# Splitting the first tap additions of a dynamic filter between GpSimd and VectorE

## The chip, the cores and the metric

The kernel runs on one core of a Trainium2 chip. Its metric is the device time of one execution in microseconds (us). The core's engines work beside each other, each through its own list of instructions in order: TensorE (PE; its weight loads stand apart as PEld), VectorE (DVE), ScalarE (ACT), GpSimd (POOL) and the queue SP, which here only issues DMAs. They wait for one another by semaphores. SBUF is the working memory; PSUM is the memory that TensorE writes[...].

## The reference: two layers on four images

The input is four images of 256 channels and 48 x 48 pixels in fp32. Layer 0 adds to each image the result of a 3x3 convolution, batch norm, ReLU and an attention over all 2304 pixels with eight heads. Layer 1 is what the change touches:

```python
def _dyn_branch(x, w, d):
    xp = jnp.pad(x, ((0, 0), (0, 0), (d, d), (d, d)))
    out = jnp.zeros_like(x)
    k = 0
    for dy in (-d, 0, d):
        for dx in (-d, 0, d):
            patch = xp[:, :, d + dy:d + dy + H, d + dx:d + dx + W]
            out = out + patch * w[:, k:k + 1]
            k += 1
    return out
guidance = _conv(x, W_cat, pad=1)
outs = [x]
for i, d in enumerate((1, 6, 12, 24, 36)):
    w = jax.nn.softmax(guidance[:, 9 * i:9 * (i + 1)], axis=1)
    outs.append(_dyn_branch(x, w, d))
y = _conv(jnp.concatenate(outs, axis=1), W_scale, pad=0)
```

So every pixel has 45 weights of its own: nine taps for each of five dilations. A tap is the image, shifted, times a weights map that is the same for all channels. The taps of a dilation are added, and a 1x1 convolution mixes the image and the five sums. A batch norm over all images follows.

## The kernel before

A tile has 128 partitions. The 256 channels are two halves of 128, which lie behind each other in a tile: a chunk of 8 image rows, 384 pixels, is 2 x 384 = 768 numbers in each partition. An image has six chunks.

The program runs image by image. The attention of an image (L951 to L1030) is followed by a stage in which `dynamic_filters` computes layer 1 of that image, while the convolution and the projections of the *next* image (L739 to L921) are mixed in between, where TensorE would else wait. There are four such stages; the last has no next image, and there the flag `alone` is set.

In a stage, each tap of a chunk goes through three engines:

- The weights map of the tap is spread over all 128 partitions into a PSUM bank, `wb`. TensorE does it with a matmul (L1384), or ScalarE copies a map that a DMA has spread (L1381). There are three such banks, five in the last stage.
- VectorE multiplies the bank with the shifted image, both halves at once. The first tap of a dilation, `at == 0`, is written straight into the sum, `cat` (L1407). Every other tap goes into one of five product buffers, `prod` (L1417), which exist so that VectorE can run ahead of GpSimd. The bank is then free.
- GpSimd adds the product to `cat`, both halves at once (L1434). The product buffer is then free.

When the last tap of a dilation has been added, TensorE mixes `cat` into the output `py` (L1280). Taps at the image's edge are smaller: with dilation 6, a tap that is shifted sideways has 42 of 48 columns, 2 x 8 x 42 = 672 numbers.

In the last stage, a product may also skip GpSimd: TensorE then mixes the product itself (`single`).

The order of all instructions is set while the program is being built. A small model, `clock`, keeps a planned time for each engine; every instruction adds its planned cost. `slot` says when a buffer comes free by that model. From these times the planner decides whether TensorE or ScalarE spreads a map, when a queued mixing matmul is due, how much of the next image's convolution goes in between (`fill`), and in the last stage which products are `single`. The planned cost of a GpSimd add is `added`. On the chip, the engines then keep that order, whatever the true times are.

Of the kernel before, what the change touches and what calls it, by code (L numbers as in the profile page):

```python
# [8 lines left out]
F32 = mybir.dt.float32  # L9
F32R = mybir.dt.float32r  # L10
AF = mybir.ActivationFunctionType
ALU = mybir.AluOpType
# [3 lines left out]
B, C, HH, WW = 4, 256, 48, 48  # L16
N = HH * WW
P = 128
NH = C // P
# [4 lines left out]
CH = R * WW  # L24
# [12 lines left out]
CATS = 4  # L37
PRODS = 5
SLACK = 3000.0
BEHIND = 0.0  # L40


# [5 lines left out]
def conv_preact_kernel(  # L48
# [12 lines left out]
    nc = tc.nc  # L61
# [73 lines left out]
    def window(gn, h, r0, dy, dx):  # L135

        return gn[:, h, 1 + r0 + dy : 1 + r0 + dy + R, 1 + dx : 1 + dx + WW]
# [393 lines left out]
    with tc.tile_pool(name="w", bufs=1) as wpool, tc.tile_pool(  # L531
        name="act", bufs=1
# [122 lines left out]
        clock = Clock()  # L655
        free = {}

        def slot(tag, bufs):

            ends = free.setdefault(tag, [])  # L660
            return ends[-bufs] if len(ends) >= bufs else 0.0
# [438 lines left out]
        def dynamic_filters(b, ao, chunk, norm, other, pools):  # L1100


            ps_w, ps_y, ps_m, work1 = pools
# [3 lines left out]
            def misc(name):  # L1107
                return ps_m.tile([P, 512], F32, tag="misc", name=name)
# [134 lines left out]
            def fill(until):  # L1243

                while clock.t["PE"] < until:
# [5 lines left out]
                    if queue and when(queue[0]) <= clock.t["PE"]:  # L1251
                        queue.pop(0)[-1]()
                        continue
                    if spent[0] > spread[0] + SLACK:
                        return
# [86 lines left out]
            for c in range(NCK):  # L1342
                if alone and c == 1:
                    back()
                if c in plan:
                    for _ in ahead:
                        pass
                    if alone and c == 2:
                        flag_of(misc("pf")[:1, : B * NH])
                    ahead = weights(plan[c])  # L1350
                    pace = [0.0, 0, 0.0]

                    due = plan[c][0] - c
                while c not in ready:
                    next(ahead)
                for o in range(NH):
                    queue.append(
                        (0.0, "", mix(c, 0, o, lambda i, c=c: window(gn, i, c * R, 0, 0)))
                    )
                w = ready[c]  # L1360
                taps = [
                    (n, at, t) for n in range(len(DILATIONS)) for at, t in enumerate(taps_of(c, n))
                ]
                for j, (n, at, (k, oy, ox, y0, y1, x0, x1)) in enumerate(taps):
                    if at == 0:
                        mixed("cat", NH * (CATS - 1))
                        cat = work1.tile(
                            [P, NH, CH], F32, tag="cat", name=f"cat_{b}_{c}_{n}", bufs=CATS
                        )
                    catv = cat.rearrange("p h (r w) -> p h r w", w=WW)  # L1370
                    nr, ncol = y1 - y0, x1 - x0
                    l0, l1 = y0 - c * R, y1 - c * R
                    fill(slot("wb", 5 if alone else 3))
                    pw = ps_w.tile([P, 512], F32, tag="w", name=f"wb_{b}_{c}_{k}")
                    spot = slot("wb", 5 if alone else 3)
                    if (c, k) in number:
                        fetch(number[c, k] + WBS)
                        of, there = landed[c, k]
                        late = max(clock.t["ACT"], spot + 150, there + 150) + 300
                    if (c, k) in number and late <= max(clock.t["DVE"], clock.t["PE"], spot + 150):  # L1380
                        nc.scalar.copy(pw[:, : nr * WW], of[:, : nr * WW])  # L1381
                        given = clock("ACT", nr * WW + 100, slot("wb", 5 if alone else 3), there)
                    else:
                        nc.tensor.matmul(  # L1384
                            pw[:, : nr * WW],
                            pick[:, k : k + 1].to_broadcast([P, P]),
                            w[:, l0 * WW : l1 * WW],
                            start=True,
                            stop=True,
                        )  # L1390
                        given = clock("PE", 0.45 * nr * WW + 20, slot("wb", 5 if alone else 3))
                    wb = (
                        pw[:, : nr * WW]
                        .rearrange("p (r w) -> p r w", w=WW)[:, :, x0:x1]
                        .unsqueeze(1)
                        .to_broadcast([P, NH, nr, ncol])
                    )
                    src = gn[:, :, 1 + y0 + oy : 1 + y1 + oy, 1 + x0 + ox : 1 + x1 + ox]
                    ns = NH * nr * ncol
                    ns, added = 1.05 * ns + 150, 2.1 * ns + (190 if ncol == WW else 80)  # L1400

                    single = (
                        alone and at > 0
                        and clock.t["POOL"] + added > clock.t["PE"] + len(queue) * NH * MM + BEHIND
                    )
                    if at == 0:
                        nc.vector.tensor_tensor(catv, wb, src, ALU.mult)  # L1407
                        end = summed = clock("DVE", ns, given)
                    else:
                        if single:  # L1410
                            mixed("single", 2 * NH)
                        tag, bufs = ("single", 3) if single else ("prod", PRODS)
                        prod = work1.tile(
                            [P, NH, CH], F32, tag=tag, name=f"prod_{b}_{c}_{k}", bufs=bufs
                        )
                        pv = prod[:, :, : nr * ncol].rearrange("p h (r w) -> p h r w", w=ncol)
                        nc.vector.tensor_tensor(pv, wb, src, ALU.mult)  # L1417
                        end = clock(
                            "DVE", ns, given, 0.0 if single else slot("prod", PRODS)
                        )  # L1420
                    free["wb"].append(end)
                    if single:
                        for o in range(NH):
                            queue.append((
                                end + 150, "single",
                                mix(
                                    c, n + 1, o,
                                    lambda i, t=prod, m=nr * ncol: t[:, i, :m],
                                    at=(l0, l1, x0, x1),
                                ),  # L1430
                            ))
                    elif at:
                        dst = catv[:, :, l0:l1, x0:x1]
                        nc.gpsimd.tensor_tensor(dst, dst, pv, ALU.add)  # L1434
                        summed = clock("POOL", added, end)
                        free["prod"].append(summed)
                    spread[0] += spread[1] * NH * nr * ncol
                    pace[0] += STEPS * 1.15 * NH * nr * ncol * NCK / due / TAP_ELEMENTS
                    if j + 1 == len(taps) or taps[j + 1][0] != n:
                        for o in range(NH):  # L1440
                            queue.append((
                                summed + 150, "cat",
                                mix(
                                    c, n + 1, o, lambda i, cat=cat: cat[:, i, :],
                                    n == len(DILATIONS) - 1,
                                ),
                            ))
# [96 lines left out]
        for b in range(B + 1):  # L1544

            with tc.tile_pool(name=f"work1_{b}", bufs=2) as work1, tc.tile_pool(
                name=f"ps_c_{b}", bufs=2, space=PSUM
            ) as ps_c, tc.tile_pool(
                name=f"ps_w_{b}", bufs=5 if b == B else 3, space=PSUM
            ) as ps_w, tc.tile_pool(  # L1550
                name=f"ps_y_{b}", bufs=1, space=PSUM
# [71 lines left out]
                else:  # L1623
                    if b == B:
# [24 lines left out]
                        def back():  # L1649

                            for bb, ty, tx in ((0, y_0, x1_0), (1, y_1, x1_1), (2, None, x1_2)):
                                if ty is not None:
                                    nc.sync.dma_start(out=ty, in_=y_d[bb])
                                nc.sync.dma_start(out=tx, in_=x1_d[bb])
                            for c, t in enumerate(y_2):
                                nc.sync.dma_start(out=t, in_=chunk_of(y_d, 2, c))
# [42 lines left out]
            with tc.tile_pool(name=f"work0_{b}", bufs=2) as work0, tc.tile_pool(  # L1699
                name=f"ps_s_{b}", bufs=3, space=PSUM  # L1700
# [3 lines left out]
                    lambda c, ao, pp, b=b, n=norm1: project(b, c, ao, pp, n), scratch,  # L1704
# [76 lines left out]
```

## Time and profile before

Three runs took 2962.0, 2967.0 and 2967.2 us. The profiled execution's span is 2967.9 us, at a mean granted TensorE clock of 0.979.

| what | instructions | busy, us | mean, ns |
|---|---|---|---|
| whole span: PE | 16967 | 2791.2 | |
| whole span: DVE | 2412 | 2390.4 | |
| whole span: ACT | 2103 | 1674.9 | |
| whole span: POOL | 1022 | 1253.5 | |
| L1434, adds on POOL | 740 | 996.5 | 1357 |
| L1417, products on DVE | 768 | 553.1 | 746 |
| L1407, first taps on DVE | 120 | 113.8 | 948 |
| L1384, maps spread by PE | 629 | 293.0 | 501 |
| L1381, maps spread by ACT | 259 | 121.2 | 468 |
| L1280, mixing of `cat` on PE | 960 | 349.6 | 496 |

The table gives busy time. A busy engine is not yet the one that sets the pace, and a share of the whole span is a mean over stages of different kinds: the four layer 1 stages lie at 559 to 854, 1277 to 1571, 1990 to 2281 and 2692 to 2930 us, some 38% of the span, and between them lie the attentions. So the questions are asked of one such stage: which engine is busy in it nearly without a gap, and who waits for whom. Matmuls are pipelined and their ends in the record are modelled, so for PE the distance from start to start says more than the busy time. The mean of a line mixes shapes of different sizes; a cost is read from the rows that keep shapes apart.

### The profile page before, as it was taken

To read this page: it belongs to the slowest core of one execution; us is meant where nothing else is said; L and a number is where in the kernel's file an instruction comes from. 1 tells how busy PE (TensorE), PEld (TensorE's weight loads), DVE (VectorE), ACT (ScalarE), POOL (GpSimd) and SP (SyncE) were. 2 spreads that over 40 slices of the span, in tenths; PEclk is the share of its full clock that TensorE was granted. 3 is DMA by queue.
4 is the path that set the end of the run, shared out by engine and by line. 5 is a ranking of instruction groups with operands and counts; after the bars stand their busy time and mean duration, and the time that the engine had idled before them with its cause. 6 is when DMAs were issued, how large, how long until landed. Compare 5 with 4: busy or idle time off the path is not lost. (4 is left out here: it accounts for less than half of the span.)

```text
span 2967.9 us, 43643 instructions
## 1 busy us (share of the span) xinstructions
PE 2791.2 (94%) x16967; PEld 1248.9 (42%) x16967; DVE 2390.4 (81%) x2412; ACT 1674.9 (56%) x2103; POOL 1253.5 (42%) x1022
## 2 busy tenths in 40 slices
PE   7999999999989999999899999999998999998994
PEld 5622224556542222455562222355555222244552
DVE  6388999779758899877976899977885999986776
ACT  3489888322348988711236988852133888871124
POOL 1010000898840010299791000069986100006994
PEclk9999999999999999999999999999999999999997
DMA  4422333222252333322225333223213333335225
GB/s 177 99 66 65 66 75 70 66 72 85 68 121 65 63 77 68 72 63 87 71 67 123 70 70 68 65 70 78 69 51 82 65 77 69 70 63 217 56 68 201
DMA packets 146232, 244.64 MB, mean 82 GB/s; under 512 B 60952, under 2 KB 111968, under 8 KB 144224
## 3 DMA queue, kind: packets, MB, share of 16 engines
q0 software_dynamic: 26720, 99.79, 15.2%
q1 hardware_dynamic: 76960, 87.31, 10.3%
q10 hardware_dynamic: 42336, 54.66, 7.0%
q8 instruction: 135, 2.21, 0.3%
q14 instruction: 81, 0.66, 0.1%
HBM read 115.02 MB, written 32.33 MB: 50 GB/s over the span
## 5 line engine op out<-in xcount | busy, mean ns | idle before, releaser
L960 ACT ACTIVATE p<-se 128x1024 f32<-128x1024 f32 x1296 | 1260.1, 1028 | 240.7 <-PE se L951 173.5
L998 DVE TENSOR_TENSOR acc<-acc,p 128x2048 f32<-128x2048 f32 (+1 forms) x572 | 1118.4, 1955 | 102.0 <-ACT p L960 55.8
L1434 POOL TENSOR_TENSOR cat<-cat,prod 128x752 f32<-128x752 f32 (+7 forms) x740 | 996.5, 1357 | 127.1 <-DVE prod L1417 86.2
L951 PE MATMUL se<-q,k 32*128 32x512 f32 (+1 forms) x5760 | 821.5, 598 | 10.7 <-DVE bound L921 6.0
L981 PE MATMUL num<-p,vT 128*32 128x512 f32 (+1 forms) x5760 | 700.0, 566 | 9.0 <-ACT scratch L1007 7.4
L1417 DVE TENSOR_TENSOR prod<-wb,pad 128x768 f32<-128x768 f32 (+7 forms) x768 | 553.1, 746 | 189.6 <-POOL cat L1434 150.5
L951 PEld LDWEIGHTS se<-q,k 32*128 32x128 f32 x5760 | 299.7, 184 | 532.9 <-issue 366.5
L1002 POOL DMA_DIRECT2D scratch<-p x144 | 122.6, 852 | 920.6 <-ACT p L960 866.2
L1280 PE MATMUL py<-cat,wsc 128*128 128x384 f32 x960 | 349.6, 496 | 18.7 <-POOL cat L1434 17.0
L1381 ACT COPY wb<-ws 128x384 f32<-128x384 f32 (+3 forms) x259 | 121.2, 468 | 423.2 <-DVE prod L1417 317.6
L981 PEld LDWEIGHTS num<-p,vT 128*32 128x32 f32 x5760 | 122.4, 108 | 492.4 <-issue 444.2
L1384 PE MATMUL wb<-w,pick 128*128 128x384 f32 (+3 forms) x629 | 293.0, 501 | 27.1 <-DVE prod L1417 24.0
L1280 PEld LDWEIGHTS py<-cat,wsc 128*128 128x128 f32 x960 | 177.9, 192 | 126.6 <-POOL cat L1434 33.0
L1000 POOL DMA_DIRECT2D scratch<-p x36 | 20.1, 558 | 470.3 <-DVE acc L998 325.1
L1384 PEld LDWEIGHTS wb<-w,pick 128*128 128x128 f32 x629 | 117.5, 192 | 152.4 <-DVE prod L1417 89.2
L850 PE MATMUL pc<-cv_q,u 128*128 128x288 f32 x576 | 159.9, 412 | 11.9 <-DVE cv_q L741 6.5
L850 PE MATMUL pc<-cv_k,u 128*128 128x288 f32 x576 | 156.4, 411 | 10.8 <-DVE yt L785 8.0
L1132 PE MATMUL pg<-pad,wcat 128*45 128x384 f32 x864 | 160.6, 504 | 1.9 <-DVE pad L591 1.8
L883 PE MATMUL pq<-hid,wqkv 128*128 128x384 f32 x384 | 136.3, 493 | 10.8 <-DVE yt L785 10.7
L850 PEld LDWEIGHTS pc<-cv_k,u 128*128 128x128 f32 x576 | 108.0, 191 | 41.8 <-DVE yt L785 10.7
L850 PEld LDWEIGHTS pc<-cv_q,u 128*128 128x128 f32 x576 | 106.9, 191 | 42.2 <-DVE cv_q L741 6.6
L1407 DVE TENSOR_TENSOR cat<-wb,pad 128x768 f32<-128x768 f32 x120 | 113.8, 948 | 10.8 <-PE wb L1384 10.7
(217 smaller groups left out, 1794.1 us busy)
## 6 DMA issues: line engine op xcount, KB each, us to landing
scratch<-p POOLq DMA_DIRECT2D x180, 512.0 KB, 4.5
ws<-w_d ACTq DMA_DIRECT2D x256, 192.0 KB, 3.2
pad<-in_x SPq DMA_DIRECT2D x14, 1152.0 KB, 15.8
u<-u_d SPq DMA_DIRECT2D x18, 768.0 KB, 4.6
x_d<-pad SPq DMA_DIRECT2D x48, 192.0 KB, 2.5
xst<-in_x SPq DMA_DIRECT2D x36, 192.0 KB, 2.4
y_d<-y SPq DMA_DIRECT2D x18, 384.0 KB, 3.1
u_d<-u SPq DMA_DIRECT2D x6, 768.0 KB, 3.7
```

The source lines that it names most:

```text
L850: nc.tensor.matmul(m, u[:, h, kx, o * P : (o + 1) * P], halves[g][:, h, i, :, kx : kx + WW], start=(h == 0 and kx == 0), stop=(h == NH - 1 ...
L883: nc.tensor.matmul(pq[:, :CH], wqkv[:, i, s, g * P : (g + 1) * P], hid[:, i, cols], start=(i == 0), stop=(i == NH - 1),)
L951: nc.tensor.matmul(ss[j // 2][:, j % 2, at : at + n], k_[r, g, m * P : (m + 1) * P], q[r, g, q0 : q0 + n], start=True, stop=True,)
L960: nc.scalar.activation(p[:, 2 * pair : 2 * pair + 2, :], ss[pair], AF.Exp, scale=QS)
L981: nc.tensor.matmul(st["num"][r, at : at + n], vT[:, m, g * P + j * D : g * P + (j + 1) * D], p[:, j, at : at + n], start=(m == 0 and not s ...
L998: nc.vector.tensor_tensor(st["acc"][:, js], other[:, js], p[:, js], ALU.add)
L1002: nc.gpsimd.dma_start(out=extra, in_=p[:, 2:], accum_op=ALU.add)
L1132: nc.tensor.matmul(pg[64 * s : 64 * s + NG, :CH], wcat[:, ii, k, :], window(gn, ii, cc * R, k // 3 - 1, k % 3 - 1), start=(i == 0 and k == 0),
L1280: nc.tensor.matmul(to, wsc[:, n * NH + i, o * P : (o + 1) * P], rhs(i), start=(n == 0 and i == 0), stop=(last and i == NH - 1),)
L1384: nc.tensor.matmul(pw[:, : nr * WW], pick[:, k : k + 1].to_broadcast([P, P]), w[:, l0 * WW : l1 * WW], start=True, stop=True,)
L1417: nc.vector.tensor_tensor(pv, wb, src, ALU.mult)
L1434: nc.gpsimd.tensor_tensor(dst, dst, pv, ALU.add)
```

## The change

From the second tap of a dilation on, as long as every earlier tap was split too (or is `single`), a tap may be *split*. It is, when GpSimd's planned time after the add would be more than 4500 ns behind VectorE's planned time. For a split tap:

- VectorE multiplies the first channel half into a product buffer, as before but half as long.
- VectorE multiplies the second half in place: the result overwrites the weights map in its PSUM bank.
- VectorE adds this result to the second half of `cat`. Only then is the bank free.
- GpSimd adds the first half alone.

Since GpSimd has not touched the second half of `cat` at that point (the rule on earlier taps sees to it), VectorE's add waits only for VectorE's own work. A later tap that isn't split is added by GpSimd in both halves, as before. The planned cost of a full add changes too: the constant 190 ns now also stands for taps of up to 36 columns, which had 80. Both together shift the planner's later decisions.

```diff
+SPLIT = 4500.0
...
-                    ns, added = 1.05 * ns + 150, 2.1 * ns + (190 if ncol == WW else 80)
+                    half = 0.525 * ns + 150
+                    ns, added = 1.05 * ns + 150, 2.1 * ns + (80 if 36 < ncol < WW else 190)
...
+                    split = (
+                        at > 0 and mine and not single
+                        and clock.t["POOL"] + added > clock.t["DVE"] + SPLIT
+                    )
+                    mine = at == 0 or split or (mine and single)
...
+                    elif split:
+                        prod = work1.tile(
+                            [P, NH, CH], F32, tag="prod", name=f"prod_{b}_{c}_{k}", bufs=PRODS
+                        )
+                        pv = prod[:, 0, : nr * ncol].rearrange("p (r w) -> p r w", w=ncol)
+                        pw = wb[:, 0]
+                        nc.vector.tensor_tensor(pv, pw, src[:, 0], ALU.mult)
+                        first = clock("DVE", half, given, slot("prod", PRODS))
+                        nc.vector.tensor_tensor(pw, pw, src[:, 1], ALU.mult)
+                        dst = catv[:, 1, l0:l1, x0:x1]
+                        nc.vector.tensor_tensor(dst, dst, pw, ALU.add)
+                        end = clock("DVE", 2 * half)
+                        dst = catv[:, 0, l0:l1, x0:x1]
+                        nc.gpsimd.tensor_tensor(dst, dst, pv, ALU.add)
+                        summed = max(clock("POOL", added / 2 + 90, first), end)
+                        free["prod"].append(clock.t["POOL"])
...
-                    elif at:
+                    elif at and not split:
                         dst = catv[:, :, l0:l1, x0:x1]
                         nc.gpsimd.tensor_tensor(dst, dst, pv, ALU.add)
```

## The prediction

> **What bounds the kernel now.** I read the page's busy shares, then its 40 slices, then busy time by stage, then the waits and the costs by shape inside one stage. The chain that ended last is no help: it holds two pieces at the very end.
>
> ```profile
> PE 2791.2 (94%) x16967; PEld 1248.9 (42%) x16967; DVE 2390.4 (81%) x2412; ACT 1674.9 (56%) x2103; POOL 1253.5 (42%) x1022
> ...
> POOL 1010000898840010299791000069986100006994
> ```
>
> Over the whole span POOL looks idle, 42%. The slices show that this is an average over two kinds of stage: 0 to 1 tenths in attention, 8 to 9 in the four stretches that the change touches. Busy time by stage (columns: stretch, its length, then PE, PEld, DVE, ACT, POOL busy, granted clock, DMA):
>
> ```profile
> 559.00:854.00 295.00, 274.74 (x1056) 168.96 (x1054) 229.66 (x337) 69.21 (x138) 264.32 (x196) 0.98 0.25 70
> 1277.00:1571.00 294.00, 271.69 (x1051) 166.25 (x1047) 228.69 (x337) 69.26 (x138) 264.65 (x196) 0.99 0.26 70
> 1990.00:2281.00 291.00, 270.88 (x1053) 166.55 (x1052) 223.54 (x325) 69.38 (x138) 265.04 (x196) 0.99 0.23 62
> 2692.00:2930.00 238.00, 225.40 (x869) 132.71 (x868) 178.92 (x261) 43.71 (x92) 217.63 (x164) 0.98 0.28 89
> ```
>
> In the first stage POOL is busy 264 of 295 us. Its successive adds lie 0.078 us apart (median of their gaps in the trace), 15 us over 195 gaps, so it needs 280 of the 291 us between its first and last instruction. PE's 274.7 us is softer: its ends are modelled. By start-to-start times (0.322 us for 384 columns, 0.161 in L1132, 0.2 for a weights matmul that waits for nothing) PE needs some 256 us. VectorE has 65 us free. Who waits, in the first stage (sum, times, longest):
>
> ```profile
> ACT wb L1381 <- DVE prod L1417: 87.3, 38, 5.5
> DVE prod L1417 <- POOL cat L1434: 40.0, 56, 1.6
> ...
> PEld wb L1384 <- DVE prod L1417: 22.3, 37, 1.2
> ...
> POOL cat L1434 <- DVE prod L1417: 16.4, 9, 3.2
> ```
>
> VectorE waits 40 us for an add to free one of the five `prod` buffers, and PE and ACT wait for VectorE to free a weights bank: the queue runs back from POOL. I paired products and adds in the trace for the 20 taps of the first stage that the change will split. The add starts 5.4 to 6.2 us after its product ended in chunks 0 to 2, 4.0 and 4.7 us in chunk 4, and 2.1 to 5.2 us in chunk 5. Through five successive taps of chunk 1, products start at 612.0, 613.7, 615.4, 617.3 and 619.0 us: VectorE, which needs 0.86 to 0.96 us each, goes at the pace of POOL. One stretch is different:
>
> ```profile
> 680.00:710.00 30.00, 28.40 (x110) 19.05 (x109) 27.32 (x41) 5.69 (x12) 27.09 (x21) 1.00 0.32 97
> 710.00:740.00 30.00, 25.50 (x92) 17.55 (x91) 29.69 (x35) 7.40 (x13) 24.10 (x16) 0.94 0.19 53
> ```
>
> Around chunk 3 VectorE is full (29.69 of 30) with the next image's convolution, and POOL starves.
>
> **What the Trainium skill says.** "GPSIMD Engine Reference", section 3.1: a two-input elementwise op costs GpSimd about twice what it costs VectorE. The trace agrees, 1830 against 952 ns for 768 elements:
>
> ```profile
> L1434 POOL TENSOR_TENSOR cat<-cat,prod 128x768 f32<-128x768 f32 x36 | 65.9, 1830 | 6.7 <-DVE prod L1417 4.1
> ...
> L1434 POOL TENSOR_TENSOR cat<-cat,prod 128x672 f32<-128x672 f32 x34 | 51.5, 1514 | 4.0 <-DVE prod L1417 1.8
> ...
> L1417 DVE TENSOR_TENSOR prod<-wb,pad 128x768 f32<-128x768 f32 x36 | 34.3, 952 | 12.8 <-POOL cat L1434 11.2 <-PE wb L1384 1.5
> ...
> L1417 DVE TENSOR_TENSOR prod<-wb,pad 128x672 f32<-128x672 f32 x34 | 28.6, 850 | 7.3 <-POOL cat L1434 7.1
> ...
> L1434 POOL TENSOR_TENSOR cat<-cat,prod 128x384 f32<-128x384 f32 x28 | 27.7, 1008 | 3.9 <-DVE prod L1417 3.2
> ```
>
> "SBUF — State Buffer", section "Who interferes with whom": a VectorE instruction with at most one SBUF input does not contend with GpSimd, one with two does. The trace fits: beside a busy POOL, L809 with both inputs in SBUF takes 1793 ns for 288 elements, L785 with one input in PSUM 446. All three new VectorE instructions have one input in PSUM, so I charge no contention. "VectorE: DVE Perf Modes", section "The DRAIN you can't avoid": a semaphore between chained VectorE ops costs nothing extra. In the trace a reciprocal that needs the transpose before it starts 0.03 us after its end, while independent products overlap by 0.08 us; so I charge 0.1 us for each self-wait.
>
> **The change part by part.** By the order of instructions, 81 taps are split: 20 in each of the first three stages, 21 in the last. In a first stage they are 5 of 768 elements, 11 of 672, 2 of 384, one of 192 and one of 168; in the last 6, 11 and 2 of the first three and 2 of 576. They lie in chunks 0, 1, 2, 4, 5 (2, 6, 5, 2 and 5 of them), none in chunk 3.
>
> *POOL, taken away.* Half an add: 768 falls from 1830 to 1008 ns (row of 384), so 0.82. 672 falls from 1514 to about 845 (interpolated between 672 and the 510 ns of the 168 form), 0.67. 384 falls from 1008 to 590, 0.42. The two small ones save 0.37 together. Sum: 5 x 0.82 + 11 x 0.67 + 2 x 0.42 + 0.37 = 12.7 us per stage. In the last stage 6 x 0.82 + 11 x 0.67 + 2 x 0.61 + 2 x 0.42 = 14.3; but the new price of narrow adds, and the shifted clock, also change which products go straight to PE. The order shows two adds more on POOL, by shapes +2.9 us, so 11.4. In all POOL loses 3 x 12.7 + 11.4 = 49.5 us.
>
> *VectorE, added.* One product becomes three half instructions. 672: 850 ns becomes 3 x 500 (between the rows of 288, 450 ns, and 384, 551 ns), +0.65. 768: 952 becomes 3 x 551, +0.70. 384: +0.5; small ones +0.4. Sum 12.5 us per stage, 13.6 in the last. Self-waits, about one per tap, +2 us. No row of before shows VectorE writing PSUM. Lower bound: as cheap as a write to SBUF, or 0.05 us less; upper bound: 0.12 us dearer, as much again as the overlap and the gap just named. I take equal. At the upper end it is 81 x 0.12 = 10 us on an engine with 65 us free per stage.
>
> *Does POOL starve?* A split tap takes VectorE 1.5 + 0.1 us against 0.85 for POOL's half add. Five in a row eat 5 x 0.75 = 3.8 of the 5.4 to 6.2 us of lag in chunks 1 and 2, so POOL keeps work. Where the lag is smaller it may starve for a while: in chunk 5 (2.1 us before three splits) and in chunk 2 of the last stage (2.0 us before five). VectorE's rise there (13 taps, 8.4 us plus waits) fits into POOL waits of 16.4 us up to 650 and 7.2 up to 740.
>
> *Weights banks.* A bank is held 1.6 us instead of 0.9. The pace at which banks come free in those runs is 1.7 us now, because VectorE waits for POOL; so PE and ACT do not wait longer. Cost zero, hidden under the POOL wait. In PSUM the half product needs no new bank.
>
> *Order.* PE has fewer convolution rows in chunk 2 (20 instead of 25) and more in chunk 3 (58 instead of 54); none falls behind the stage's last mixing matmul, before or after. DMA queues: SP's order is unchanged, ACT copies one more weights map, PE makes one fewer. Zero.
>
> *Sum.* Chunks 0 to 2 take 7.8 us from POOL, of which I count 6: PE, needing about nine tenths of that time, can't follow wholly. Chunk 3 is VectorE's; the shifted convolution costs 1. Chunks 4 and 5 take 4.9, of which 3.5. That is 8.5 per stage, 25.5 for three. In the last stage two thirds of 11.4, 7.5. Total 33 us: 2967.9 - 33 = 2935. The profiled run's 2967.9 stands within 0.2% of the median of 2967.0 and of the lowest, 2962.0.
>
> **Rivals.** *PE takes over (0.18).* For: PE's modelled busy is 93% of the stage, and weights matmuls that follow a wait start late (0.38 us median spacing, not 0.2). Against: it needs 256 of 295 by spacing. Then each stage gives 3 us, 12 in all: 2956. *All of POOL's time comes back (0.08).* 49.5 us: 2918. Against: chunk 3. *No change that can be told (0.05).* The splits merely move POOL's idle time into chunk 3 and to the stage ends: 2967. It would need every other chunk to be VectorE-bound, which 40 us of POOL waits deny. *Slower (0.12): banks held too long.* PE issues in order, and convolution and mixing matmuls queue behind a weights matmul that waits for its bank. If the 0.7 us that a bank is held longer reached PE at every split tap, it would be 20 x 0.7 = 14 us more waiting per stage; with PE's present 20 us of idle needed for its other waits, the stage would grow to 295 + 14 - 8.5 = 300, and four of them give 2987. It decides from 8.5 us per stage, 0.43 us per split tap. Against it stands the 1.7 us pace.
>
> **How the numbers follow.** Forecast 0.57 (2924 to 2947). The range from 2920 to 2960 holds it, the PE case and part of the full one; outside lie most of the slower case, no change, and the far end of the full gain, about 0.2. A measurement of this kernel tells about 0.2%, 6 us, from nothing. Faster: 0.57 + 0.18 + 0.08 = 0.83; same 0.05; slower 0.12.
>
> **What would show it.** POOL's busy time falls by about 12 us in a stage and by 49 in all, VectorE's rises by about as much; VectorE's wait for POOL falls from 40 us towards 20; the stages shorten to about 286, 285, 282 and 230 us, with their ends moving in chunks 1, 2, 4 and 5. Wrong would be: the new VectorE triple far over 1.7 us, PE's wait for weights banks well above the 22 us of now, or POOL idle in the split chunks.

## The result and the profile after

The changed kernel takes 2929.0 us (median of four runs, 2926.9 to 2933.6) against 2967.1 us: ratio 0.9878, 95% interval 0.9861 to 0.9895. It is 38 us faster; 2935 was forecast.

The page of the changed kernel, to be held against the two lines of before:

```profile
PE 2773.1 (95%) x16950; PEld 1246.7 (43%) x16950; DVE 2426.1 (83%) x2574; ACT 1675.2 (57%) x2104; POOL 1205.2 (41%) x1024
...
POOL 1010010898840010299791100059986010005894
```

POOL lost 48.3 us of busy time and VectorE gained 35.7, with 162 more instructions. By stage (columns as before):

```profile
555.00:839.00 284.00, 269.66 (x1055) 167.56 (x1054) 238.18 (x377) 69.41 (x138) 251.70 (x196) 0.99 0.27 73
1262.00:1546.00 284.00, 269.83 (x1056) 167.72 (x1054) 237.98 (x377) 69.28 (x138) 251.84 (x196) 0.99 0.27 73
1969.00:2249.00 280.00, 268.50 (x1055) 167.41 (x1053) 231.97 (x366) 69.37 (x138) 251.75 (x196) 0.99 0.24 65
2660.00:2890.00 230.00, 216.50 (x854) 129.14 (x852) 189.85 (x304) 44.20 (x94) 206.32 (x166) 0.99 0.31 93
```

From here on, a stage is measured from the first L1407 product (L1416 in the changed kernel) to its last mixing matmul. The four went from 293.8, 293.9, 290.2 and 238.2 us to 282.8, 282.8, 278.9 and 229.6: 42.0 us in all. The rest of the profiled span went from 1851.8 to 1853.5 us. That part differs by up to 12 us between the profiled executions of all kernels below, and this sets a limit to reading single spans.

Waits in the first stage of the changed kernel:

```profile
ACT wb L1382 <- DVE prod L1442: 60.1, 29, 4.9
...
PEld wb L1385 <- DVE prod L1442: 18.5, 29, 1.9
POOL cat L1459 <- DVE prod L1442: 18.0, 12, 3.2
DVE prod L1442 <- POOL cat L1459: 15.2, 21, 1.6
```

VectorE's wait for GpSimd fell from 40.0 to 15.2 us. GpSimd's wait for VectorE hardly rose, 16.4 to 18.0, so it was not starved. The waits for a weights bank did not grow either, though a split tap holds it longer: with every VectorE instruction that frees a bank counted, ScalarE's fell from 88.4 to 67.8 us, and those of PE's weight loads from 24.4 to 23.4.

The new instructions, by shape, in the first stage:

```profile
L1426 DVE TENSOR_TENSOR wb<-wb,pad 128x336 f32<-128x336 f32 x11 | 5.6, 505 | 0.0
L1428 DVE TENSOR_TENSOR cat<-cat,wb 128x336 f32<-128x336 f32 x11 | 5.5, 504 | 0.4
L1424 DVE TENSOR_TENSOR prod<-wb,pad 128x336 f32<-128x336 f32 x11 | 5.5, 502 | 0.2
...
L1428 DVE TENSOR_TENSOR cat<-cat,wb 128x384 f32<-128x384 f32 x5 | 2.8, 554 | 0.2
...
L1431 POOL TENSOR_TENSOR cat<-cat,prod 128x336 f32<-128x336 f32 x11 | 9.2, 837 | 0.5
```

Overwriting the weights in PSUM costs 505 ns, writing to SBUF 502. And this is the pace of one split tap, on VectorE's timeline (start, length):

```profile
612.14 0.50 DVE L1424 TENSOR_TENSOR prod<-wb,pad 128x336 f32<-128x336 f32 x1
612.55 0.51 DVE L1426 TENSOR_TENSOR wb<-wb,pad 128x336 f32<-128x336 f32 x1
613.10 0.51 DVE L1428 TENSOR_TENSOR cat<-cat,wb 128x336 f32<-128x336 f32 x1
613.52 0.50 DVE L1424 TENSOR_TENSOR prod<-wb,pad 128x336 f32<-128x336 f32 x1
```

From product to product 1.38 us pass. The in-place product starts 0.09 us before the record of the one ahead ends; the add, which waits for its own engine's result, 0.04 us after.

### The profile page after: what moved, and what is told of

Same layout as the page of the kernel before. It is cut to its first block, busy times and chain, and to the rows that moved or that the text cites. A ratio compares the mean times of both kernels' runs of the same rounds, so it can differ in the third digit from the quotient of the medians.

```text
span 2927.6 us, 43833 instructions
## 1 busy us (share of the span) xinstructions
PE 2773.1 (95%) x16950; PEld 1246.7 (43%) x16950; DVE 2426.1 (83%) x2574; ACT 1675.2 (57%) x2104; POOL 1205.2 (41%) x1024
## 5 line engine op out<-in xcount | busy, mean ns | idle before, releaser
L1459 POOL TENSOR_TENSOR cat<-cat,prod 128x752 f32<-128x752 f32 (+9 forms) x661 | 883.1, 1345 | 133.6 <-DVE prod L1442 96.7
L952 PE MATMUL se<-q,k 32*128 32x512 f32 (+1 forms) x5760 | 819.6, 596 | 12.5 <-ACT p L961 6.2
L1442 DVE TENSOR_TENSOR prod<-wb,pad 128x384 f32<-128x384 f32 (+8 forms) x687 | 483.4, 738 | 94.4 <-POOL cat L1459 55.9
L1385 PE MATMUL wb<-w,pick 128*128 128x384 f32 (+3 forms) x628 | 299.7, 509 | 24.7 <-DVE prod L1442 15.8
L1416 DVE TENSOR_TENSOR cat<-wb,pad 128x768 f32<-128x768 f32 x120 | 114.0, 950 | 11.4 <-PE wb L1385 10.8
```

The source lines that it names most:

```text
L952: nc.tensor.matmul(ss[j // 2][:, j % 2, at : at + n], k_[r, g, m * P : (m + 1) * P], q[r, g, q0 : q0 + n], start=True, stop=True,)
L1385: nc.tensor.matmul(pw[:, : nr * WW], pick[:, k : k + 1].to_broadcast([P, P]), w[:, l0 * WW : l1 * WW], start=True, stop=True,)
```

## The experiments

Theory A is that of the prediction: GpSimd sets the pace of most chunks, and time taken from it there comes off the stage. Rivals: B, the new order and the new price do it; C, VectorE's added work takes back a good part; D, the place of the second product does not matter; E, PE or VectorE bounds the stages already. Each kernel was timed in several rounds beside the kernel before on the same chip; ratios are to that kernel, with 95% intervals. The edits are shown against the changed kernel, unless the text says otherwise.

**Only the price of a narrow add.**

```diff
-SPLIT = 4500.0
+SPLIT = 1e9
```

> No tap is split; only the planned price of an add of up to 36 columns is changed, and with it the order. Theory A (the gain is GpSimd time taken out of stretches in which GpSimd sets the pace): GpSimd's work is unchanged at 740 adds, so 2960 to 2972 us, and POOL busy 264 us in the first stage. Rival B (the gain comes from the planner's better price and the order that follows): most of the 38 us is here already, 2930 to 2945.

2967.2 us, ratio 1.0005 (0.9996 to 1.0014); POOL busy in the first stage:

```profile
557.00:851.00 294.00, 272.18 (x1055) 168.47 (x1053) 228.37 (x337) 69.50 (x139) 265.49 (x197) 0.99 0.24 70
```

The price and the order that follows from it alone bring nothing. B falls, in its simple form.

**The split within the order of before.** The edit is against the kernel before. The taps are given as a list, `TAPS`, and the planner's clock books them as if they were whole; 80 come to be split.

```diff
+                    split = at > 0 and mine and not single and (b, c, k) in TAPS
+                    mine = at == 0 or split or (mine and single)
...
+                        nc.vector.tensor_tensor(pv, pw, src[:, 0], ALU.mult)
+                        nc.vector.tensor_tensor(pw, pw, src[:, 1], ALU.mult)
+                        dst = catv[:, 1, l0:l1, x0:x1]
+                        nc.vector.tensor_tensor(dst, dst, pw, ALU.add)
+                        end = clock("DVE", ns, given, slot("prod", PRODS))
...
-                        dst = catv[:, :, l0:l1, x0:x1]
+                        dst = catv[:, 0 if split else slice(None), l0:l1, x0:x1]
```

> The order and every choice of before, on TensorE and ScalarE instruction for instruction, and 80 taps split within it. Theory A: POOL loses 12.7 us per stage as in the change, and the order is a minor matter: 2928 to 2940 us, three quarters of the gain or more. Rival B: without the new order little is gained, 2955 to 2968.

2935.4 us, ratio 0.9890 (0.9875 to 0.9905). With TensorE's and ScalarE's lists unchanged, 31 of the 38 us are there. GpSimd's busy time in the first stage is close to that of the changed kernel:

```profile
556.00:843.00 287.00, 269.36 (x1057) 168.18 (x1055) 238.13 (x378) 68.84 (x138) 253.25 (x197) 0.99 0.25 72
```

The stages are 285.6, 285.4, 281.8 and 230.4 us. So the split carries the gain. Planning with it adds some 6 us by the medians, for which the prediction had nothing; the two intervals overlap, but each stage of the profiled runs points the same way (together 1083.2 us against 1074.1).

**The split with the old price.**

```diff
-                    ns, added = 1.05 * ns + 150, 2.1 * ns + (80 if 36 < ncol < WW else 190)
+                    ns, added = 1.05 * ns + 150, 2.1 * ns + (190 if ncol == WW else 80)
```

> The split with the old price of a narrow add: the planner then sees GpSimd less behind and splits 67 taps, not 81. Theory A: the gain goes with the GpSimd time taken away, 67/81 of 38 us is 31, so 2931 to 2940. Rival B: the price carries the gain, so 2950 to 2967.

2925.6 us, ratio 0.9855 (0.9839 to 0.9872), with 67 splits. It is below the range of A, 2931 to 2940: 14 splits fewer gained at least as much (the intervals of the two kernels overlap). So the gain is not in proportion to the number of splits. Measured to GpSimd's last add of each chunk in the first stage, 6.7 of the 13.8 us that the stage gains over the kernel before lie in chunk 3, where it splits two taps and the changed kernel none; why chunk 3 shortens so much, no run here shows. The run speaks against B, which expected 2950 or more, and only in part for A.

**VectorE's work and the long hold of the bank, without relief for GpSimd.**

```diff
+                        pv = prod[:, :, : nr * ncol].rearrange("p h (r w) -> p h r w", w=ncol)
+                        nc.vector.tensor_tensor(pv[:, 1], pw, src[:, 1], ALU.mult)
                         nc.vector.tensor_tensor(pw, pw, src[:, 1], ALU.mult)
-                        dst = catv[:, 1, l0:l1, x0:x1]
-                        nc.vector.tensor_tensor(dst, dst, pw, ALU.add)
...
-                        dst = catv[:, 0, l0:l1, x0:x1]
+                        dst = catv[:, :, l0:l1, x0:x1]
                         nc.gpsimd.tensor_tensor(dst, dst, pv, ALU.add)
```

> The order of the change, and VectorE does three half operations at each of the 81 taps (two products into the product buffer, and one more in place in the weights bank that nobody reads), but GpSimd adds both halves as before. It tells VectorE's price and the longer hold of the bank from the relief of GpSimd. Theory A: the gain is gone, 2960 to 2975 us, POOL busy again 264 us per stage. If the order, or VectorE's pieces themselves, brought the gain (rival B), 2930 to 2945. If VectorE's 0.65 us and the held bank cost much once GpSimd gives no relief (rival C), 2980 or more.

2976.2 us, ratio 1.0030 (1.0021 to 1.0038), 1 us beyond the range of A:

```profile
556.00:850.00 294.00, 270.54 (x1057) 168.00 (x1055) 237.87 (x378) 69.03 (x138) 264.54 (x196) 0.99 0.25 71
```

VectorE is as busy as in the changed kernel (237.87 against 238.18), GpSimd as busy as before (264.54), and the gain is gone. The order is the changed kernel's, planned for shorter adds; how much of the 9 us of loss is that misfit and how much VectorE's price, this run does not tell.

**VectorE's second half left out.**

```diff
-                        nc.vector.tensor_tensor(pw, pw, src[:, 1], ALU.mult)
-                        dst = catv[:, 1, l0:l1, x0:x1]
-                        nc.vector.tensor_tensor(dst, dst, pw, ALU.add)
```

> As the change, in its order, but the second channel half of the 81 taps is left out: VectorE does one half product instead of three half operations, GpSimd adds one half. The sums lack that half. Theory A: VectorE's 1.0 us per split tap is hidden under its waits for GpSimd, except near chunk 3 where VectorE is full; 2920 to 2929 us, so at most 9 us below the change. Rival C (VectorE's added work takes back a good part of the relief): 2900 to 2915.

2933.2 us, ratio 0.9885 (0.9870 to 0.9900), 4 us above the range of A. VectorE loses 15 us in the first stage and nothing becomes faster:

```profile
557.00:840.00 283.00, 269.23 (x1054) 167.36 (x1052) 222.74 (x337) 68.77 (x138) 251.35 (x196) 0.99 0.26 73
```

The four stages sum to 1076.2 us against 1074.1. VectorE's added work in the changed kernel is hidden, as far as these runs can tell; C falls.

**The second product in SBUF.**

```diff
-                        nc.vector.tensor_tensor(pw, pw, src[:, 1], ALU.mult)
+                        pu = prod[:, 1, : nr * ncol].rearrange("p (r w) -> p r w", w=ncol)
+                        nc.vector.tensor_tensor(pu, pw, src[:, 1], ALU.mult)
                         dst = catv[:, 1, l0:l1, x0:x1]
-                        nc.vector.tensor_tensor(dst, dst, pw, ALU.add)
+                        nc.vector.tensor_tensor(dst, dst, pu, ALU.add)
```

> As the change, but VectorE's second product goes to the free half of the product buffer in SBUF instead of over the weights in PSUM, and VectorE's add reads two SBUF inputs. The bank comes free one instruction (0.5 us) earlier. Theory A with contention: VectorE's 81 adds, beside a busy GpSimd, take far longer than 0.50 us (before, L809 with two SBUF inputs took 1.79 us for 288 elements), and GpSimd may slow down too: 5 to 25 us slower than the change, 2934 to 2955. Rival D (where the product lies does not matter, and the longer hold of the bank costs something): equal or faster, 2922 to 2931.

2947.3 us, ratio 0.9941 (0.9929 to 0.9953): 18 us slower than with the product in PSUM. VectorE's add and GpSimd's half add by shape, first stage:

```profile
L1429 DVE TENSOR_TENSOR cat<-cat,prod 128x336 f32<-128x336 f32 x11 | 10.5, 956 | 0.4
L1429 DVE TENSOR_TENSOR cat<-cat,prod 128x384 f32<-128x384 f32 x5 | 6.2, 1237 | 0.2
...
L1432 POOL TENSOR_TENSOR cat<-cat,prod 128x336 f32<-128x336 f32 x11 | 10.7, 970 | 0.5
```

The add of 336 takes 956 ns instead of 504, that of 384 takes 1237 instead of 554, and GpSimd's 837 become 970. This is what "SBUF — State Buffer", section "Who interferes with whom", of the Trainium skill says of two SBUF inputs beside GpSimd, here with a size. The kernel before has a control for it. L809 has two SBUF inputs in every one of its 16 executions. It took 457 to 459 ns the four times that GpSimd was idle (74 to 83 us), and 1628 to 1958 ns the twelve times within the layer 1 stages:

```profile
L809 DVE TENSOR_TENSOR cs<-cs x16: 457/1638/1958, 74.3 to 2153.7; 128x288 f32<-128x288 f32 x16
```

D falls: the place in PSUM is worth about half of the gain. GpSimd's adds take 13.4 us longer in all (969.0 against 955.6 us); how the 18 us divide between that and VectorE's longer adds was not tested.

**More splits.** The threshold alone is changed, to 3000 and to 1500 ns.

> The threshold at 3000 ns instead of 4500: 140 taps are split. Theory A, as long as GpSimd sets the pace: another 59 taps take some 38 us from GpSimd, but PE needs 256 of then about 275 us in a stage and VectorE about 255, so only a third to a half comes through: 2905 to 2922 us. Rival E (VectorE or PE bounds the stages already after the change): 2924 to 2940.

> The threshold at 1500 ns: 251 taps are split. VectorE gains about 0.65 us per tap, 110 us more than in the change over four stages, 27 per stage on top of 238 of 284 us: VectorE now sets the pace in most chunks and GpSimd idles. Theory A: no better than with 3000, 2915 to 2950 us. If GpSimd were still the bound, 2890 or less.

With 3000: 2920.9 us, ratio 0.9848 (0.9835 to 0.9860), in the range of A. With 1500: 2956.7 us, ratio 0.9972 (0.9961 to 0.9983), 7 us above the expected range. The first stage with 1500, and GpSimd's largest wait there:

```profile
559.00:847.00 288.00, 270.34 (x1055) 168.25 (x1053) 254.10 (x463) 69.58 (x138) 224.25 (x196) 0.99 0.25 72
...
POOL cat L1459 <- DVE prod L1442: 38.2, 33, 4.5
```

With 1500, GpSimd is down to 224 us of 288 and waits 38 us for VectorE's full products (and 12 more for half ones), which the added work now holds up. The gain turns round between 140 and 251 splits.

**What bounds the stages after the change.** GpSimd adds one channel half only of the taps that aren't split:

```diff
-                        dst = catv[:, :, l0:l1, x0:x1]
-                        nc.gpsimd.tensor_tensor(dst, dst, pv, ALU.add)
+                        dst = catv[:, 0, l0:l1, x0:x1]
+                        nc.gpsimd.tensor_tensor(dst, dst, pv[:, 0], ALU.add)
```

> The order and all VectorE work of the change, but GpSimd adds only the first channel half of the taps that are not split, so the sums lack their second half. GpSimd falls from some 249 to about 150 us per stage and cannot set any pace. It tells what bounds the stages once GpSimd is out of the way. If GpSimd still sets the pace after the change, much is left: 2860 to 2895 us. If PE and VectorE are already close (256 us and 238 us of 283 by the traces), 2900 to 2920, about 3 to 7 us per stage below the change.

2859.8 us, ratio 0.9636 (0.9623 to 0.9649). The stages fall to 261.1, 261.1, 260.4 and 224.6 us, and GpSimd is now the one that waits:

```profile
POOL cat L1459 <- DVE prod L1442: 85.7, 80, 3.7
```

The first three stages lose 18.5 to 21.7 us each, so as a statement on whole stages E falls there. In the last stage only 5 us are left. What remains in the first, 261 us, is near the 256 us that the start-to-start times gave for PE.

By chunk the picture is finer. Measured to GpSimd's last add of each chunk in the first stage, chunk 0 gives 6.6 us, chunks 1 and 2 together 0.1, chunk 3 10.3, chunks 4 and 5 together 7.0, and 2.3 are lost after the last add. (Measured to the first product of each chunk on VectorE, chunks 1 and 2 give 0.6 us and chunk 3 11.9.) In chunks 1 and 2, which hold 11 of the stage's 20 splits, halving GpSimd's adds brings next to nothing, so GpSimd has ceased to set the pace there, and E fits. These are the two chunks in the changed kernel (columns as before):

```profile
600.40:644.00 43.60, 43.55 (x190) 25.05 (x188) 36.74 (x63) 10.02 (x23) 40.89 (x36) 1.00 0.32 84
644.00:687.70 43.70, 42.61 (x181) 25.16 (x178) 37.49 (x64) 8.10 (x17) 41.90 (x32) 1.00 0.32 93
```

PE's record has hardly a gap in chunk 1, but its ends are modelled; whether PE is the bound there, no run tests. In chunk 3 the run changes a second thing: VectorE's instructions with two SBUF inputs become cheaper beside a GpSimd that is busy less. The same line, in the first stage of the changed kernel and of this run:

```profile
L810 DVE TENSOR_TENSOR cs<-cs x4: 1640/1863/1953, 689.7 to 714.2; 128x288 f32<-128x288 f32 x4
...
L810 DVE TENSOR_TENSOR cs<-cs x4: 457/718/981, 686.4 to 707.0; 128x288 f32<-128x288 f32 x4
```

L781 and L810 together fall from 22.0 to 11.1 us. How much of chunk 3's 10.3 us is GpSimd's pace and how much VectorE's cheaper work, this run does not tell.

**Versions in between.** The old price with thresholds of 3000 and 3750, the new one with 3750.

> The old price of a narrow add, threshold 3000: 128 taps split. The price alone changed nothing, and with threshold 4500 it gave 2925.6 us with 67 splits. Theory A: GpSimd loses some 30 us more than in that run; with PE close, a quarter of it arrives: 2914 to 2922 us. If VectorE or the order already bounds: 2922 to 2932.

> The old price, threshold 3750, between the two: 2916 to 2926 us.

> The new price, threshold 3750: 124 taps split, between the change (81 taps, 2929.0 us) and the threshold of 3000 (140 taps, 2920.9 us): 2918 to 2928 us.

| price, threshold | splits | us | ratio, 95% interval |
|---|---|---|---|
| old, 3000 | 128 | 2913.8 | 0.9821 (0.9807 to 0.9834) |
| old, 3750 | 95 | 2921.6 | 0.9843 (0.9830 to 0.9857) |
| new, 3750 | 124 | 2919.9 | 0.9841 (0.9828 to 0.9855) |

The first beats both kernels: 15 us below the change, and just below its expected range. Its runs spread widely, 2907.8 to 2919.9 us. Its stages sum to 1062.3 us against 1074.1; the rest of the 15 us lies outside the stages, where it can't be put down to the split.

## Why the prediction was right, point by point

- *GpSimd sets the pace.* Right for the kernel before, by two runs together: its work taken away without a new order (31 us), VectorE's new work without relief (no gain). Still less of its work brings 69 us more, of which a part may be VectorE's cheaper work in chunk 3.
- *POOL's time taken away.* Forecast 12.7 us per stage and 11.4 in the last. The adds went from 261.7 to 249.1 us in the first stage and from 219.5 to 208.1 in the last: 12.6 and 11.4. The interpolated 845 ns for 336 elements was 837.
- *VectorE's added time.* The three durations were right (500 forecast, 502 to 505 measured), and writing PSUM costs the same. Their sum as time on the engine was too large: 14.5 us per stage forecast, 8.5 measured. A slip of addition is in it (the parts listed for a first stage make 12.1 us, not 12.5), but the most of it is that I had summed whole durations and put 0.1 us on each self-wait; independent operations start before the record of the one ahead ends, and a split tap takes 1.38 us, not 1.6. It made no difference, since the run without this work is no faster.
- *Banks.* Cost zero: right. PE's weight loads waited 23.4 us for VectorE to free a bank, where they had waited 24.4.
- *What arrives of it.* Measured to GpSimd's last add of each chunk from the stage's start, chunks 0 to 2 gave 6.9 us in the first stage (139.2 to 132.3) and 8.2 in the second and third (140.5 to 132.3); I had 6. Chunk 3 took back at most 1.2; I had 1. Chunks 4 and 5 gave 4.0; I had 3.5. The three stages gave 11.0, 11.1 and 11.3 us instead of 8.5, the last 8.6 instead of 7.5. But within the order of before, nearly the same time taken from GpSimd gave 8.2, 8.5, 8.4 and 7.8. So the discount for what PE and chunk 3 don't let through came out right in sum. By chunk there is luck in it: chunks 0 to 2 gave 3.8, 6.4 and 6.6 there, chunks 4 and 5 gave 4.2 to 4.4, and chunk 3 took back up to 2.4.
- *Order.* I took zero; by the medians this is the term that was too small. Between the split in the old order and the change lie 2.6 to 2.9 us in each of the first three stages and 0.8 in the last, 9 us of the profiled stages and some 6 of the whole time. Which part of the new order brings it was not tested, and the new price without splits brought nothing. It is about the 6 us by which the forecast was off.
- *The rivals.* PE as the new bound would have given 2956, with 3 us per stage. After the change more relief for GpSimd brings next to nothing in chunks 1 and 2, where PE may be the bound, but by then a stage has gained 11 us. The slower case needed 0.43 us of waiting per split tap at PE, some 8.5 us per stage; the waits for banks did not grow.

## What to carry to other kernels

An engine with 42% of the span can set the pace where it counts: ask by stage, and count its fixed gaps too. After the change ask again, by chunk: the stage as a whole still answered to less GpSimd work, the two chunks with most of the splits no longer did. To relieve it, give the neighbour only as much as fits its waits, and stop before the roles turn round; here that is between 140 and 251 of 740 adds. Where two engines contend for SBUF, moving one input to a PSUM buffer that is about to be dropped can be worth as much as the split itself, as it was here.

## What the runs showed of the hardware

VectorE overwrites a PSUM operand in place at the price of a write to SBUF: 505 against 502 ns for 336 elements, 556 against 550 for 384. An add with both inputs in SBUF beside a busy GpSimd took 1.9 to 2.2 times as long as the same add with one input in PSUM, and slowed GpSimd's add by 16% (837 to 970 ns). A subtraction of 288 elements with two SBUF inputs (L809 before, L810 after) took 457 to 459 ns in all its 17 executions with no GpSimd add beside it, and 975 to 1958 ns in the other 31, in the traces of before, of the change and of the run with half of GpSimd's adds.
